# Four graph layers on one core: the first two graphs' layernorm and the linear part of their elu move to VectorE, and a planner gets other durations for transfers

## The chip, the core and the metric

The kernel runs on one core of a Trainium2 chip. The core has five engines that work side by side and each take their instructions in the order in which the program lists them: TensorE (PE: matrix products and transposes into PSUM, with weight loads of its own, PEld), VectorE (DVE), ScalarE (ACT), GpSimd (POOL) and SyncE (SP), which here issues nearly all DMA transfers. The metric is the device time of one execution in microseconds (us), the median of several runs; lower is better.

## The reference

The input is 32 graphs of 512 nodes with 128 features in fp32, and one 512x512 adjacency matrix of zeros and ones that all graphs share. Four residual layers follow each other, each on `h = relu(layernorm(x))`:

```python
# layer 0, on h; the part that the change touches
x_h = elu(h @ Wi + bi)                                  # one 128x512 product a graph
a_src, a_tgt = x_h @ We[:H, 0], x_h @ We[H:, 0]
e = sigmoid(a_tgt[:, :, None] + a_src[:, None, :] + be) * mask
agg = e @ x_h;  self_part = x_h * e.sum(-1)
recv = elu(concat(agg, self_part) @ Wn + bn)
x = x + concat(recv, x_h) @ Wm + bm
# layer 1: five steps of a gated update  h = (1-z) h + z tanh(...), each with adj @ h
# layer 2: x + adj @ (h W) + b
# layer 3: x + sum over k of (adj^k @ h) V_k, k = 0..3
```

## The kernel before

**Layout.** A graph's activations are one tile of 128 features by 512 nodes (or 128 nodes by 4 chunks of 128 features). Graphs are taken in eight groups of four (`G = 4`); layers 0, 1 and 2 are done graph by graph, layer 3 for a group at once. Buffers are numbered slots: 36 SBUF tiles of 128x512 (`f`), and PSUM banks (`b`, eight, of which one is lent to filler work at first).

**The order is written by a planner.** All work is first listed as operations (`op`, line 59) with an engine, a planned duration `us`, a due time, what they read and write, and `result`, the time after its end at which others are thought to see its result (2.5 us for a transfer of SP unless another is given, 0.2 us for the vector engines). `Plan.order` (line 118) then runs through planned time: whenever an engine is free, it takes the ready operation with the earliest due time whose buffers are free. What comes out is a fixed order for each engine, and a fixed slot for each tile. On the chip each engine simply works through its list and waits, with semaphores, for what an instruction needs. A planned duration therefore costs no time itself; it only moves instructions in the lists. A longer `result` puts the consumer later in its engine's list.

**Two plans.** The first covers planned time up to `BRANCH = 18` us (`plan.order(end=BRANCH)`, line 692). In it, when TensorE has nothing ready, a filler product of `ones` by `ones` is written into its list (`plan.idle`, line 301). Then a branch on whether the adjacency matrix is exact in the short format (`inexact`) chooses one of two arms, and the rest is planned for that arm (line 704), without filler.

**The start.** SP issues the loads in the order of their due times: graphs 0 and 1, `Wi`, `bi`, the four chunks of the adjacency matrix, graph 2, and the other weights (lines 313 to 353). The adjacency matrix is transposed, and `mask` is made from it (lines 500 to 531); `n_odd` counts entries that the short format can't hold, and `inexact` is made from the count. In `layernorm` (line 465) VectorE makes the moments (lines 474 to 477), GpSimd the power -1/2 (line 479), VectorE a shift (line 482) and ScalarE, with four instructions of 128x128, `relu(x * scale + shift)` (line 487).

**Layer 0** (`layer0`, line 549), for the first four graphs without DMA: TensorE transposes `h` (line 371), ScalarE copies it from PSUM (line 431), TensorE multiplies by `Wi` (line 442). `elu` (line 534) is three ScalarE instructions on the product, exp (538), tanh (447) and relu (541), and two on VectorE (543, 545). `send` (568) makes messages and scores; `take` (573) and `score` (575) get them out of PSUM; `spread` (605) broadcasts the target scores. Four tanh (620) and four products with `mask` (623) give the attention tiles `es`. They are multiplied by the messages into `pn` (631), and summed over the sources into `ps`: for the first two graphs by four fp32 products with `ones` (line 638, seen at L442), for all others by transfers: SP copies the first tile (641), three accumulating transfers of GpSimd's queue add the others (644), ScalarE and VectorE split the sum in two short parts (648, 649), and TensorE makes the total (654). Then `own` (657), the product with `Wn` (seen at L442), a second `elu`, the output product (667) and the addition to x (462).

Due times in `layer0` are `begin(b)` plus 6, 14, 20, 30 and 44 us; `begin(b)` is 14 us times b for the first four graphs.

Of the kernel before, what the change touches and what calls it, by code (L numbers as in the profile page):

```python
# [13 lines left out]
AF = mybir.ActivationFunctionType  # L14
ALU = mybir.AluOpType

P = 128
# [24 lines left out]
class Plan:  # L42
# [7 lines left out]
    def __init__(self, slots, ahead, last):  # L50
        self.ahead, self.last, self.ops, self.vals = ahead, last, [], {}
        self.free = {k: [(0.0, i) for i in range(n)] for k, n in slots.items()}
        self.until = dict.fromkeys(self.RESULT, 0.0)
        self.shared, self.now = 0.0, 0.0
        self.slack = 0.0
        self.pieces = {}
        self.idle = None
# [60 lines left out]
    def order(self, end=None):  # L118
# [34 lines left out]
        while events:  # L153
# [3 lines left out]
            for e in self.until:  # L157
# [12 lines left out]
                for x in passed:  # L170
                    heapq.heappush(ready[e], x)
                if o is not None and end is not None and any(
                    c.due < o.due and t < now + 0.3 * o.us for t, _, c in coming[e]
                ):
                    heapq.heappush(ready[e], (o.due, index[o], o))
                    o = None
# [37 lines left out]
def tile_four_graph_layers(  # L214
# [97 lines left out]

    def load(v, src, due, us=0.5, to=None, earliest=0.0):
        op("SP", us, due, lambda: nc.sync.dma_start(at(v) if to is None else to(at(v)), src), [], [v],
           earliest=earliest)
        return v

    def load_const(src, shape, name, due, us=0.5, earliest=0.0):
        return load(const(name, shape), src, due, us, earliest=earliest)

    def load_column(src, name, due):
        return load_const(src.rearrange("(p o) -> p o", o=1), [P, 1], name, due, 0.4)

# [5 lines left out]

    def load_graph(b, due):  # L330
        op("SP", 0.65, due, lambda: nc.sync.dma_start(
            at(X[b]), x[b].rearrange("(c p) d -> p c d", p=P)),
            [], [X_group[b // G], X[b]] if b % G == 0 else [X[b]])
# [12 lines left out]
    load(W_tok, Wn[:P], -7, to=lambda t: t[:, :P])  # L346
    load(W_tok, We.rearrange("(t p) o -> p (t o)", p=P), -7, to=lambda t: t[:, P:])
    be_sb = load_const(be.partition_broadcast(P), [P, 1], "be_sb", -7)
    Wn_sb = load_const(Wn[P:], [P, P], "Wn_sb", -6)
    bn_sb = load_column(bn, "bn_sb", -6)  # L350
    Wm_sb = load_const(Wm.rearrange("(t p) o -> p t o", p=P), [P, 2, P], "Wm_sb", -5)
    bm_bc = load_const(bm.partition_broadcast(P), [P, P], "bm_bc", -5, earliest=BRANCH)
    load_graph(3, -6)

# [109 lines left out]

    def layernorm(b, due):
# [25 lines left out]
        op("ACT", 1.56, due, scale, [X[b], s], [h])  # L491
        return h
# [40 lines left out]

    def elu(p, bias, half, due, keep, scale=1.0):

# [13 lines left out]
    def layer0(b, h, due):  # L549
        KEEP = 12  # L550
        if b < G:
            hT = copied(transposed(h, due), due)
        else:
            hT = turned_back(h, due)
            due += 6
        d = due + 6
        xhT = elu(product(Wi_sb, hT, d, blocks=b >= G), bi_sb, bi_half, d, KEEP)

        d = due + 14
        msg, ends = Val("f"), Val("s")  # L560
# [21 lines left out]

        d = due + 20
        row, tgt = Val("d"), Val("f")
# [42 lines left out]

        d = due + 30
        pn = Val("b")
# [49 lines left out]
    def first_layer(b):  # L679
        h = layernorm(b, begin(b))  # L680
        layer0(b, h, begin(b))
# [316 lines left out]
```

## Time and profile before

| what | us |
|---|---|
| median of 3 runs | 1678.89 (1675.96 to 1679.08) |
| the profiled execution | 1678.16 |
| its span in the profile | 1676.4 |
| PE busy | 1662.9 |
| DVE busy | 1420.3 |
| ACT busy | 1130.5 |
| POOL busy | 239.6 |

The profiled execution took 1.8 us more than its span, which is what lies ahead of the first and after the last instruction. It was 0.7 us under the median of the runs. PE's busy time counts the filler too, and matmuls overlap in it, so that a busy PE isn't one that does useful work all the time; where it loses time has to be counted from the starts of its instructions. The granted TensorE clock was 0.999 of full speed.

### The profile page before, as it was taken

To read this page: it belongs to the slowest core of one execution; us is meant where nothing else is said; L and a number is where in the kernel's file an instruction comes from. 1 tells how busy PE (TensorE), PEld (TensorE's weight loads), DVE (VectorE), ACT (ScalarE), POOL (GpSimd) and SP (SyncE) were. 2 spreads that over 40 slices of the span, in tenths; PEclk is the share of its full clock that TensorE was granted. 3 is DMA by queue.
4 is the path that set the end of the run, shared out by engine and by line. 5 is a ranking of instruction groups with operands and counts; after the bars stand their busy time and mean duration, and the time that the engine had idled before them with its cause. 6 is when DMAs were issued, how large, how long until landed. Compare 5 with 4: busy or idle time off the path is not lost.

```text
span 1676.4 us, 21509 instructions
## 1 busy us (share of the span) xinstructions
PE 1662.9 (99%) x6615; PEld 1073.7 (64%) x6615; DVE 1420.3 (85%) x3327; ACT 1130.5 (67%) x2145; POOL 239.6 (14%) x243
## 2 busy tenths in 40 slices
PE   9999999999999999999999999999999999999998
PEld 7555555556666666666666666666666666666797
DVE  6888999999988888889888898888999988877742
ACT  8877677876875676656676676665777767655541
POOL 2311101211111111111101111111121110000110
PEclk9999999999999999999999999999999999999999
DMA  3444424444445434444434444344554543222301
GB/s 108 114 107 138 134 88 138 121 130 115 134 113 138 120 96 127 110 122 131 121 106 111 130 127 127 107 123 109 135 138 122 138 111 103 88 64 88 93 10 53
DMA packets 284157, 188.05 MB, mean 112 GB/s; under 512 B 77312, under 2 KB 236928, under 8 KB 284032
## 3 DMA queue, kind: packets, MB, share of 16 engines
q1 hardware_dynamic: 271072, 162.98, 32.5%
q0 software_dynamic: 12960, 23.60, 8.5%
q8 instruction: 54, 0.88, 0.2%
q14 instruction: 71, 0.58, 0.1%
HBM read 82.25 MB, written 72.81 MB: 92 GB/s over the span
## 4 chain that ended last, share of the span: by engine, by line
PE 62%; DMA 2%; DVE 1%; ACT 0%; issue 0%; SPq 0%; DVEq 0%; POOLq 0%
PE b L442 27%; PE b L821 13%; PE b L911 9%; PE b L902 5%; PE b L631 3%; PE b L667 2%; PE b L884 1%; DMA f<-f 1%; PE b L568 1%; DMA m<-f 1%; PE b L654 1%; DMA f<-m 0%; DVE f L383 0%; SPq L420 0%; ACT f L620 0%
## 5 line engine op out<-in xcount | busy, mean ns | idle before, releaser
L821 PE MATMUL b<-AQ,r 128*128 128x512 f32 x1024 | 303.8, 439 | 0.0
L431 ACT COPY f<-b 128x512 f32<-128x512 f32 x360 | 207.9, 586 | 120.6 <-PE b L821 87.2
L479 POOL TENSOR_TENSOR s<-s,nhalf 128x4 f32<-128x4 f32 x128 | 154.8, 1212 | 822.0 <-DVE s L477 702.6
L821 PEld LDWEIGHTS b<-AQ,r 128*128 128x128 f32 x1024 | 192.3, 188 | 89.3 <-issue 51.5
L846 DVE TENSOR_TENSOR f<-f,b 128x512 f32<-128x512 f32 x320 | 210.9, 676 | 26.6 <-PE b L442 26.2
L911 PE MATMUL b<-r,A_r 128*128 128x512 f32 x768 | 225.0, 427 | 0.0
L383 DVE STREAM_TRANSPOSE f<-f 128x512 f32<-128x512 f32 x244 | 204.7, 843 | 21.2 <-ACT f L487 20.4
L487 ACT ACTIVATE f<-x,s 128x128 f32<-128x128 f32 x512 | 210.5, 490 | 17.4 <-DVE s L482 16.9
L447 ACT ACTIVATE f<-f,b4w 128x512 f32<-128x512 f32 x160 | 115.4, 723 | 144.1 <-DVE f L846 143.5
L911 PEld LDWEIGHTS b<-r,A_r 128*128 128x128 f32 x768 | 139.0, 189 | 46.2 <-issue 24.4
L442 PE MATMUL b<-f,u5T 128*128 128x512 f32 x320 | 163.3, 593 | 1.0 <-DVE f L853 1.0
L442 PE MATMUL b<-f,u3T 128*128 128x512 f32 x320 | 163.3, 593 | 1.0 <-DMA f<-m 1.0
L442 PE MATMUL b<-f,w4T 128*128 128x512 f32 x320 | 162.8, 592 | 0.0
L442 PE MATMUL b<-f,w3T 128*128 128x512 f32 x320 | 162.4, 592 | 0.0
L442 PE MATMUL b<-f,w5T 128*128 128x512 f32 x320 | 162.4, 592 | 0.0
L644 POOL DMA_DIRECT2D f<-f x90 | 80.7, 896 | 536.4 <-DVE f L865 58.1
L821 PE MATMUL b<-A_r,r 128*128 128x512 f32 x512 | 151.9, 438 | 0.0
L863 DVE TENSOR_TENSOR f<-f,f 128x512 f32<-128x512 f32 x160 | 109.2, 683 | 48.9 <-ACT f L447 48.4
L902 PEld LDWEIGHTS b<-V,f 128*128 128x128 f32 x1024 | 131.4, 191 | 25.6 <-issue 19.9
L447 ACT ACTIVATE f<-b,b5w 128x512 f32<-128x512 f32 x160 | 109.4, 684 | 56.0 <-PE b L442 53.5
L447 ACT ACTIVATE f<-f,b3w 128x512 f32<-128x512 f32 x160 | 114.9, 719 | 43.1 <-DVE f L846 42.2
L795 DVE TENSOR_TENSOR r<-f,r 128x512 fp32r<-128x512 f32 x192 | 130.5, 682 | 12.6 <-ACT r L791 12.4
(106 smaller groups left out, 2539.3 us busy)
## 6 DMA issues: line engine op xcount, KB each, us to landing
m<-f SPq DMA_DIRECT2D x244, 256.0 KB, 2.1
f<-m SPq DMA_DIRECT2D x184, 256.0 KB, 2.9
f<-f POOLq DMA_DIRECT2D x90, 256.0 KB, 3.6
f<-m SPq DMA_DIRECT2D x240, 64.0 KB, 2.4
x<-in_x_dram SPq DMA_DIRECT2D x32, 256.0 KB, 3.2
out_dram<-x SPq DMA_DIRECT2D x32, 256.0 KB, 2.5
f<-f SPq DMA_DIRECT2D x30, 256.0 KB, 2.3
f<-d SPq DMA_DIRECT2D x28, 256.0 KB, 5.1
```

The costliest lines, as they stand in the source:

```text
L383: op("DVE", us, due, lambda: nc.vector.transpose(view_out(at(blocks)), view_in(at(src))), [src], [blocks])
L431: op("ACT", us, due, lambda: nc.scalar.copy(at(t), at(src)), [src], [t])
L442: nc.tensor.matmul(to, at(w), of, start=start, stop=stop)
L447: op("ACT", us, due, lambda: nc.scalar.activation(at(dst), at(src), AF.Tanh, bias=at(bias), scale=scale), [src, bias], [dst])
L479: op("POOL", 1.35, due, lambda: nc.gpsimd.tensor_tensor(stat(SCALE), stat(VAR), at(neg_half), op=ALU.pow), [s, neg_half], [s])
L487: nc.scalar.activation(at(h)[:, ts(c, P)], at(X[b])[:, c, :], AF.Relu, bias=stat(SHIFT)[:, c : c + 1], scale=stat(SCALE)[:, c : c + 1],)
L795: op("DVE", T_VEC, due, lambda: nc.vector.tensor_tensor(part(lo), whole(), part(hi).bitcast(F32), op=ALU.subtract), [src, hi], [lo], two=two)
L821: nc.tensor.matmul(at(pa), at(part)[:, ts(jc, P)], view(at(columns)[:, jc, :]), start=jc == n == 0, stop=jc == NC - 1 and n == PARTS - 1,)
L846: op("DVE", T_VEC, d, lambda: nc.vector.tensor_tensor(at(s), at(u), at(pg), op=ALU.add), [u, pg], [s])
L863: op("DVE", T_VEC, d, lambda c=c, h=h: nc.vector.tensor_tensor(at(c), at(c), at(h), op=ALU.subtract), [c, h], [c], two=True)
L902: nc.tensor.matmul(at(pz)[:, ts(i, D)], at(hT[i])[:, ts(ic, P)], at(V[k]), start=i == 0, stop=last and i == G - 1,)
L911: nc.tensor.matmul(at(pz), at(adjT)[:, jc, ts(ic, P)], at(part), start=False, stop=jc == NC - 1 and n == PARTS - 1,)
```

## The change

It has six parts.

1. For graphs 0 and 1 (`FIRST = 2`), `layernorm(relu=False)` leaves out the shift and the four ScalarE instructions; VectorE makes `(x - mean) * scale` in four instructions, and the relu is put into the copy of the transposed tile from PSUM, which stays on ScalarE.
2. In the first `elu` of these two graphs, the linear part `max(p + bias, 0)` is made by VectorE instead of ScalarE.
3. Due times in layer 0 of these two graphs are 0.6 of what they were, and the products with `ones` are due 1 us ahead of the products with the messages. The moments of the first four graphs aren't planned ahead of `begin(b) - 12`.
4. Loads get a shorter time to issue (0.48) and a `result` of their own each.
5. The accumulating transfers get `result=4.6` instead of 3.0, for graphs 2 to 31.
6. In the planner, an operation's ready time is now an event at which the plan looks again, and the rule by which an engine waits for a more urgent operation holds while planned time is under `careful = 18.0` instead of while there is an `end`.

```diff
-                if o is not None and end is not None and any(
+                if o is not None and now < self.careful and any(
                     c.due < o.due and t < now + 0.3 * o.us for t, _, c in coming[e]
...
                             heapq.heappush(coming[a.eng], (a.ready, index[a], a))
+                            heapq.heappush(events, a.ready)
...
+    FIRST = 2
...
+    plan.careful = 18.0
...
-    def load(v, src, due, us=0.5, to=None, earliest=0.0):
+    def load(v, src, due, us=0.5, to=None, earliest=0.0, result=None):
...
-        op("SP", 0.65, due, lambda: nc.sync.dma_start(
+        op("SP", 0.48, due, lambda: nc.sync.dma_start(
...
-    load_graph(0, -9)
-    load_graph(1, -9)
+    load_graph(0, -9, 2.5)
+    load_graph(1, -9, 2.9)
...
-        load(A_nat[ic], adj[ts(ic, P), :], -8, 0.65)
-    load_graph(2, -8)
+        load(A_nat[ic], adj[ts(ic, P), :], -8, 0.48, result=3.9 + 0.2 * ic)
+    load_graph(2, -8, 4.8)
...
-        op("DVE", 1.3, due, moments, [X[b]], [s])
+        op("DVE", 1.3, due, moments, [X[b]], [s], earliest=earliest)
...
-        op("DVE", 0.1, due, lambda: nc.vector.scalar_tensor_tensor(
-            stat(SHIFT), mean(), -1.0, stat(SCALE), op0=ALU.mult, op1=ALU.mult),
-            [s], [s], two=True)
+        if relu:
+            op("DVE", 0.1, due, lambda: nc.vector.scalar_tensor_tensor(
+                stat(SHIFT), mean(), -1.0, stat(SCALE), op0=ALU.mult, op1=ALU.mult),
+                [s], [s], two=True)
...
+        def normed():
+            for c in range(NC):
+                nc.vector.tensor_scalar(
+                    at(h)[:, ts(c, P)], at(X[b])[:, c, :], mean()[:, c : c + 1],
+                    stat(SCALE)[:, c : c + 1], op0=ALU.subtract, op1=ALU.mult)
+        if relu:
+            op("ACT", 1.56, due, scale, [X[b], s], [h])
+        else:
+            op("DVE", 0.9, due, normed, [X[b], s], [h])
...
-        op("ACT", T_ACT, due, lambda: nc.scalar.activation(
-            at(r), at(p), AF.Relu, bias=at(bias), scale=scale), [p, bias], [r])
+        if relu_by_vector:
+            assert scale == 1.0
+            op("DVE", T_VEC, due, lambda: nc.vector.tensor_scalar(
+                at(r), at(p), at(bias), 0.0, op0=ALU.add, op1=ALU.max), [p, bias], [r])
+        else:
+            op("ACT", T_ACT, due, lambda: nc.scalar.activation(
+                at(r), at(p), AF.Relu, bias=at(bias), scale=scale), [p, bias], [r])
...
-            hT = copied(transposed(h, due), due)
+            pt, hT = transposed(h, due), Val("f")
+            op("ACT", T_COPY, due, lambda pt=pt: nc.scalar.activation(
+                at(hT), at(pt), AF.Relu if b < FIRST else AF.Copy), [pt], [hT])
...
-        d = due + 6
-        xhT = elu(product(Wi_sb, hT, d, blocks=b >= G), bi_sb, bi_half, d, KEEP)
-
-        d = due + 14
+        pace = 0.6 if b < FIRST else 1.0
+        d = due + 6 * pace
+        xhT = elu(product(Wi_sb, hT, d, blocks=b >= G), bi_sb, bi_half, d, KEEP,
+                  relu_by_vector=b < FIRST)
+
+        d = due + 14 * pace
...
-        d = due + 20
+        d = due + 20 * pace
...
-        d = due + 30
+        d = due + 30 * pace
...
-                product(ones, es[jc], d, ps, start=jc == 0, stop=jc == NC - 1)
+                product(ones, es[jc], d - 1, ps, start=jc == 0, stop=jc == NC - 1)
...
-                   two=False, result=3.0)
+                   two=False, result=4.6)
...
-        recv = elu(pn, bn_sb, bn_half, d + 6, 2, ALPHA / 2)
-
-        d = due + 44
+        recv = elu(pn, bn_sb, bn_half, d + 6 * pace, 2, ALPHA / 2)
+
+        d = due + 44 * pace
...
-        h = layernorm(b, begin(b))
+        h = layernorm(b, begin(b), relu=b >= FIRST, earliest=begin(b) - 12.0 if b < G else 0.0)
```

The other loads get their `result` in the same way (W_tok 4.5, be 4.3, Wn 4.0, bn 3.6, graph 3 3.6), and columns are issued in 0.48 instead of 0.4.

More of the change, by code (lines that the diff above doesn't have):

```diff
@@ L54, in __init__ @@
         self.shared, self.now = 0.0, 0.0
+        self.careful = 0.0
         self.slack = 0.0
@@ L310, in tile_four_graph_layers, with load_const, load_column @@
         at(warm)[:, :1], at(ones)[:, :1], AF.Tanh), [ones], [warm])
-    def load(v, src, due, us=0.5, to=None, earliest=0.0):
+    def load(v, src, due, us=0.5, to=None, earliest=0.0, result=None):
         op("SP", us, due, lambda: nc.sync.dma_start(at(v) if to is None else to(at(v)), src), [], [v],
-           earliest=earliest)
+           earliest=earliest, result=result)
         return v
[L318 to L322, printed above, removed]
+    def load_const(src, shape, name, due, us=0.5, earliest=0.0, result=None):
+        return load(const(name, shape), src, due, us, earliest=earliest, result=result)
+    def load_column(src, name, due, result=None):
+        return load_const(src.rearrange("(p o) -> p o", o=1), [P, 1], name, due, 0.48, result=result)
     X_group = [Val("x") for _ in range(NG)]
@@ L328, in tile_four_graph_layers, with load_graph @@
     plan.vals.update(dict.fromkeys([*X_group, *X]))
-    def load_graph(b, due):
-        op("SP", 0.65, due, lambda: nc.sync.dma_start(
+    def load_graph(b, due, result=None):
+        op("SP", 0.48, due, lambda: nc.sync.dma_start(
             at(X[b]), x[b].rearrange("(c p) d -> p c d", p=P)),
-            [], [X_group[b // G], X[b]] if b % G == 0 else [X[b]])
-    load_graph(0, -9)
-    load_graph(1, -9)
+            [], [X_group[b // G], X[b]] if b % G == 0 else [X[b]], result=result)
+    load_graph(0, -9, 2.5)
+    load_graph(1, -9, 2.9)
     Wi_sb = load_const(Wi, [P, P], "Wi_sb", -9)
@@ L340, in tile_four_graph_layers @@
     for ic in range(NC):
-        load(A_nat[ic], adj[ts(ic, P), :], -8, 0.65)
-    load_graph(2, -8)
+        load(A_nat[ic], adj[ts(ic, P), :], -8, 0.48, result=3.9 + 0.2 * ic)
+    load_graph(2, -8, 4.8)
     W_tok = const("W_tok", [P, P + 2])
-    load(W_tok, Wn[:P], -7, to=lambda t: t[:, :P])
+    load(W_tok, Wn[:P], -7, to=lambda t: t[:, :P], result=4.5)
     load(W_tok, We.rearrange("(t p) o -> p (t o)", p=P), -7, to=lambda t: t[:, P:])
-    be_sb = load_const(be.partition_broadcast(P), [P, 1], "be_sb", -7)
-    Wn_sb = load_const(Wn[P:], [P, P], "Wn_sb", -6)
-    bn_sb = load_column(bn, "bn_sb", -6)
+    be_sb = load_const(be.partition_broadcast(P), [P, 1], "be_sb", -7, result=4.3)
+    Wn_sb = load_const(Wn[P:], [P, P], "Wn_sb", -6, result=4.0)
+    bn_sb = load_column(bn, "bn_sb", -6, result=3.6)
     Wm_sb = load_const(Wm.rearrange("(t p) o -> p t o", p=P), [P, 2, P], "Wm_sb", -5)
     bm_bc = load_const(bm.partition_broadcast(P), [P, P], "bm_bc", -5, earliest=BRANCH)
-    load_graph(3, -6)
+    load_graph(3, -6, 3.6)
     def scaled(v, factor, name, due):
@@ L463, in add_to_x, with layernorm @@
         op("DVE", T_VEC, due, add, [X[b], p], [X[b]], two=two)
-    def layernorm(b, due):
+    def layernorm(b, due, relu=True, earliest=0.0):
         s, h = Val("s"), Val("f")
@@ L490, in scale @@
                 )
-        op("ACT", 1.56, due, scale, [X[b], s], [h])
+        def normed():
[7 more added lines that the diff above has]
+            op("DVE", 0.9, due, normed, [X[b], s], [h])
         return h
@@ L531, in tile_four_graph_layers, with elu @@
        [p_odd], [inexact])
-    def elu(p, bias, half, due, keep, scale=1.0):
+    def elu(p, bias, half, due, keep, scale=1.0, relu_by_vector=False):
         e, t, r = Val("f"), Val("f"), Val("f")
```

## The prediction, made before the changed kernel was run

> **What bounds the kernel now.** I read the busy time of the engines first, then TensorE's waits, then the waits of the engines that feed it, then the first 60 us as a timeline and by stretches. The page's first part:
>
> ```profile
> PE 1662.9 (99%) x6615; PEld 1073.7 (64%) x6615; DVE 1420.3 (85%) x3327; ACT 1130.5 (67%) x2145; POOL 239.6 (14%) x243
> ```
>
> TensorE is the bound, but its busy time holds filler and overlap. So I count useful work: an fp32 product with 512 columns is two matmul records 0.429 us apart, a record in the short format 0.231, a 128-column fp32 record 0.112 (differences of starts in the timeline). Over all rows but the filler this makes 1643.0 us. Up to a time t, the lost time is t less the useful work begun by then: 15.3 us at 20, 16.1 at 25, 16.4 at 45, 17.1 at 55, 18.3 at 100, 27.0 at 1600. After the last matmul come 6.4 us (last addition, store). So only two things can give time back: 18 us at the start, and scattered stalls, which the waits of TensorE name:
>
> ```profile
> PE b L654 <- DVE q L649: 2.8, 5, 0.9
> PE b L301 <- DVE ones L296: 1.0, 1, 1.0
> PE b L442 <- DVE f L853: 1.0, 2, 0.6
> PE b L442 <- DMA f<-m: 1.0, 1, 1.0
> PE b L631 <- DVE f L623: 0.6, 1, 0.6
> PE b L442 <- DVE f L657: 0.5, 2, 0.3
> ```
>
> The largest is the total of the attention tiles, which waits for the accumulating transfers by way of two engines. The same wait on those engines, in the list for all engines:
>
> ```profile
> ACT q L648 <- DMA f<-f: 29.9, 19, 4.9
> ...
> DVE q L649 <- ACT q L648: 16.3, 13, 2.6
> ```
>
> In 19 of 30 graphs ScalarE stands still for the last accumulation, and all that is listed behind L648 stands too. The transfers (last row on L644) land in
>
> ```profile
> DMA to landing us min/median/max: 3.2/3.6/4.9
> ```
>
> The start by stretches (columns: PE, PEld, DVE, ACT, POOL busy, clock, DMA):
>
> ```profile
> 10.00:20.00 10.00, 10.00 (x90) 9.37 (x90) 8.03 (x30) 8.37 (x19) 1.90 (x4) 1.00 0.09 21
> 20.00:30.00 10.00, 9.36 (x38) 4.95 (x37) 7.21 (x31) 9.87 (x24) 3.69 (x8) 1.00 0.53 138
> 30.00:40.00 10.00, 9.90 (x39) 5.48 (x38) 8.38 (x21) 10.00 (x24) 1.04 (x1) 1.00 0.22 68
> ```
>
> From 20 to 40 us ScalarE is full (9.87, 10.00): it feeds TensorE there. Before that, TensorE's timeline:
>
> ```profile
> 9.60 0.72 PE L301 MATMUL b<-ones 128*128 128x128 f32 x5
> 10.16 1.47 PE L513 MATMUL b<-ident,f 128*128 128x128 f32 x12
> 11.47 0.60 PE L371 MATMUL b<-ident,f 128*128 128x128 f32 x4
> ```
>
> The first 31 fillers end at about 10.1 us, and real work waits for them in the list: the last chunk of the adjacency matrix landed at 9.0, and graph 0's `h` was done at 9.8 (L487, 8.14 plus 1.64).
>
> **What the Trainium skill says.** "TensorE: Matmul & The Clock Gate", Architectural detail: ScalarE's and VectorE's queues are strict FIFO. The trace agrees: L648's 29.9 us. "ScalarE: Activation LUTs", What ACT_TABLE_LOAD costs: an ACTIVATE with a pointer operand takes about 280 + 0.833 N ns, 93 more for a second one, and neighbours overlap by 93, so an estimate of 0.39 us for each step of L487; in the trace four stand in 1.55 us (25.08 to 26.63), the same. "VectorE: DVE Perf Modes", The TRN2 errata: (58 + N/2)/0.96 ns for fp32 `tensor_scalar` in SBUF at double rate, (120 + N)/0.96 from PSUM at single rate. "DMA: Bandwidth & Descriptors", Anatomy of one DMA: 2.0 us + bytes/436e3, an estimate of 2.6 us for 256 KB from GpSimd; the trace has 3.6, and the trace decides.
>
> **The change, part by part.**
>
> *Off ScalarE.* For two graphs L487 (2 x 1.55) and L541 (2 x 0.57 start to start): 4.2 us, and two L482 (0.15 each) off VectorE. *Onto VectorE:* eight 128x128 `tensor_scalar`, which the trace hasn't got. From below, the skill's price (58 + 64)/0.96 = 127 ns each, 0.5 us a graph; from above the nearest row, L474 at 0.87 for four. I take 0.8. For the relu the price is 0.66, the row L543 0.69, 0.61 start to start. The relu in the copy costs nothing: the same instruction count, 0.59 as L431. Nothing here is on the path at first: VectorE is done with graph 0 at about 7.1 us (pow ends at 6.15), while fillers cover TensorE until 10.1, as they cover 9.8 now. Without them it would save 2.7 us. What is listed behind the new VectorE steps, the checks of the adjacency chunks, waits for ScalarE's casts until 7.6 anyway.
>
> *Order at the start.* The changed program lists 55 fillers (53 before, 0.22 us each), the first 31 again ahead of everything, then graph 0's transposes before the adjacency ones. I laid its lists end to end with the durations above (0.47 for a copy on ScalarE, 0.57 for exp or tanh, 0.58 a tanh of the attention, 0.61 on VectorE, 1.27 for moments, 0.2 from VectorE or ScalarE to TensorE), each instruction starting when its engine and its inputs allow:
>
> - Graph 0: transposes 10.16 (11.47 now), `Wi` product 11.7 (13.0), messages 16.4 (17.1; five fillers stand ahead of them), target scores 18.3 (19.9), first tanh of the attention 18.9 (20.6). A lead of 1.6 us.
> - Then the lists spend it. Graph 1's `Wi` product, at 20.4 now, stands behind the four products with `ones` (20.7 to 24.1, as fast as VectorE delivers) and starts at 24.1. ScalarE, done with graph 1's copy at 21.8, has nothing until 25.2: 3.4 idle us in the stretch that it fills now, of the 4.2 that it was relieved of.
> - First stall: graph 1's scores go to the bank that holds graph 0's `pn`, which ScalarE reads last at 31.46; TensorE is there at 30.6, starts at 31.66: 1.05 us. Second: the output product of graph 0 waits for its second `elu`, whose last VectorE step stands behind moments of two later graphs and ends at 34.4; TensorE is there at 32.9, starts at 34.6: 1.7. Third: graph 0's first product of layer 1 goes to the bank that graph 2's relu reads until 47.3; TensorE is there at 46.6: 0.9.
> - At 53.8 us the useful work begun is 34.4: lost 19.4, against 17.0 or 17.1 now. So +2.3 us, and I take no more until 100 us, as now 1.3 is lost there. The method may be off by 2 us either way: ScalarE's list is the chain, and 0.05 us on each of its 60 instructions makes 3.
>
> *Loads as planned.* SP's list keeps its first 16 transfers in the same order, so nothing lands at another time. `inexact` is made about 3 us sooner (16 instead of 19.1), so the loads behind the branch (now from 20.3) go about 3 us sooner, too, into an idle queue: no cost; nothing waits for them.
>
> *Accumulation, 4.6 instead of 3.0.* Three accumulations follow each other: planned 3 x (1.0 + 3.0) = 12.0 us, now measured steps of 4.05 and 3.77 (issues at 49.54, 53.59, 57.36), in the tail up to 4.9 + 0.5 each. Planned after: 16.8. In the listed order, the useful TensorE work between a graph's scores and its L654 grows from 29 to 35 us at the least, 32.5 to 38 in the middle. The worst stall now is 1.02 us (at 640.8), so 4.8 more cover all. That removes L654's later stalls, counted from starts with the next instruction's delay: 0.75 (323.6), 0.73 (386.0), 0.38 (581.3), 1.02 (640.8), 0.65 (1147.1), and 0.43 on the product after it (643.2): 3.96. Buffers are held 4.8 us longer in a queue of 36; the listed work shows no thinner place.
>
> *New event.* It lets the plan start work up to 0.3 us sooner, all through. The gates of layer 1 get tighter: the useful work between the w4 and u5 products, with add, tanh and multiply (L846, L447, L853) between, is at most 3.6 us in 12 places instead of 5. A stall there costs 0.75 (at 633.1). I take +0.7. The `careful` edit changes nothing, as both hold exactly in the first plan.
>
> Sum: +2.3 - 4.0 + 0.7 = -1.0, on the profiled 1678.16: 1677.2; that execution stands 0.7 under the median, so I say 1677.5. A measurement of this kernel can tell about 0.2%, 3.4 us.
>
> **Rivals.**
>
> *The start pays as meant.* ScalarE is full from 20 to 40 us, so 4.2 us less there could all come back as TensorE time: -4.2 - 3.3 = -7.5, 1670.7; half of it, 1674.2. For it: the first graph's lead of 1.6 us. Against: the 3.4 us hole behind the `ones` products.
>
> *The gates of layer 1 take it all.* 0.75 us for each tight place: if the 7 more all stall, +5.3, and with the start +2.3 and -4.0: +3.6, 1681.8. It decides from seven on (+3.4 with rounding). For it: VectorE is 85% busy and its list is in order. Against: of the five places now, the two stalls seen (62.5 and 633.1, 1.3 us) are not at the tightest.
>
> *The later sum doesn't help, since `own` and the `Wn` product move along with it.* The distance from L654 to the product is 1.7 us as before. Then only the start stays, +2.3 to +3: 1680.5 to 1681, still same. Against: that distance is as short now, and only two of the 30 products stalled.
>
> **How the numbers follow.** The mixed outcome (near nothing, the last rival with it) 0.52; the start pays 0.28; the gates or a worse start 0.20. Its own range is 1675.0 to 1681.5. To hold eight in ten I reach to most of the first rival, 1671.0, and past the second, 1683.5.
>
> **What would show it.** Right: L654 missing from TensorE's waits after 100 us, L648's 29.9 us down to a few; ScalarE idle about 3 us between 21 and 26 us; stalls at L628 (scores), L690 (output product) and L844 (layer 1), by the changed file's lines, between 30 and 50 us; lost time near 19 at 55 us. Wrong: graph 1's `Wi` product before 22 us; no stall until 50; or waits on L876 (now L853) summing to over 3 us.

## The result, and the profile after

The changed kernel takes 1681.91 us (median; 1680.43 to 1683.72), the kernel before 1678.09 on the same chip: a ratio of 1.0023, with a 95% interval of 1.0015 to 1.0032. The forecast was 1677.5, so the time lies within the range on record, but some 4 us above the forecast: the kernel became a little slower instead of staying as it was. The profiled execution has a span of 1679.9 us (1676.4 before). Useful TensorE work is the same 1643.0 us in both; all that moved is lost time. The first part of the page of the changed kernel shows TensorE at 99% again, with 1.7 us less "busy" although the kernel is slower, which is why lost time is counted from the starts of matmuls:

```profile
PE 1661.2 (99%) x6619; PEld 1075.8 (64%) x6619; DVE 1424.3 (85%) x3335; ACT 1127.9 (67%) x2135; POOL 236.9 (14%) x243
```

Lost time (t less the useful work begun by t, as in the prediction), by stretch:

| stretch | before | after | difference | predicted |
|---|---|---|---|---|
| to 55 us | 17.1 | 18.9 | +1.8 | +2.3 |
| 55 to 100 us | 1.2 | 3.1 | +1.9 | 0 |
| 100 to 400 us | 3.7 | 6.4 | +2.7 | |
| 400 to 1600 us | 5.0 | 1.8 | -3.2 | -3.3 for both stretches |

The tail behind the last matmul is 0.8 us longer (7.2 against 6.4), and 0.4 less is lost between 1600 us and it. The waits of TensorE in the changed kernel (total us, times, longest), to be read against those of before: the attention total, there the largest with 2.8 us in five places, is left with one wait (L677, at 78 us, in graph 2). Line numbers moved with the change: the total is L654 in the kernel before and L677 in the changed one (L655 and L676 in some files below), while L654 of the changed kernel is the product of the attention with the features. That product and the u3 product (L447 with L890; u3, u5 and w4 are products of layer 1's gated steps) stand in the total's place:

```profile
PE b L654 <- DVE f L646: 2.3, 2, 1.8
PE b L447 <- DVE f L890: 2.0, 1, 2.0
PE b L628 <- ACT f L560: 1.7, 1, 1.7
PE b L447 <- DMA f<-m: 1.3, 1, 1.3
PE b L677 <- DVE q L672: 1.1, 1, 1.1
...
PE b L844 <- ACT f L560: 0.7, 1, 0.7
PE b L690 <- DVE f L564: 0.6, 1, 0.6
```

L628, L844 and L690 are the three stalls of the start that the prediction named. ScalarE's wait for the accumulating transfers, 29.9 us before, is gone from the list altogether; VectorE's wait behind it fell from 16.3 us to

```profile
DVE q L672 <- ACT q L671: 3.9, 6, 0.8
```

The start on TensorE's timeline (start, length, line; in brackets the idle time and what ended it). Graph 1's first product, behind eight records with `ones`, begins at 24.05, and the three stalls follow at 32.36, 34.37 and 47.33:

```profile
20.61 3.60 PE L447 MATMUL b<-f,ones 128*128 128x512 f32 x8
24.05 1.02 PE L447 MATMUL b<-f,Wi_sb 128*128 128x512 f32 x2
...
32.36 0.65 PE L628 MATMUL b<-ident,s 128*128 128x128 f32 x4 [1.67 <-ACT f L560]
...
34.37 2.05 PE L690 MATMUL b<-Wm_sb,f 128*128 128x128 f32 x16 [0.58 <-DVE f L564]
...
47.33 2.14 PE L844 MATMUL b<-A_r,r 128*128 128x512 f32 x8 [0.74 <-ACT f L560]
```

ScalarE's timeline shows the pause foretold (3.39 us), and a second wait that was not:

```profile
25.11 0.69 ACT L552 ACTIVATE f<-b,bi_sb 128x512 f32<-128x512 f32 x1 [3.39 <-PE b L447]
26.62 0.69 ACT L452 ACTIVATE f<-b,bi_half 128x512 f32<-128x512 f32 x1 [0.82 <-DVE f L557]
```

L452 reads the bank that L557, the new relu on VectorE, reads as well. Here the two readers went one after the other.

Further on, the largest new stall is the one at 330.37 us on a u3 product, 2.15 us. VectorE's timeline ahead of it (start, length, line):

```profile
327.18 0.71 DVE L388 STREAM_TRANSPOSE f<-f 128x512 f32<-128x512 f32 x1
327.81 0.65 DVE L888 SCALAR_TENSOR_TENSOR f<-f,f 128x512 f32<-128x512 f32 x1
328.38 0.86 DVE L479 BATCH_NORM_STATS2 s<-x 128x6 f32<-128x128 f32 x4
329.15 0.36 DVE L481 BATCH_NORM_AGGREGATE s<-s 128x2 f32<-128x6 f32 x4
329.55 0.17 DVE L482 TENSOR_SCALAR s<-s 128x4 f32<-128x4 f32 x1
329.63 0.68 DVE L890 SCALAR_TENSOR_TENSOR f<-f,f 128x512 f32<-128x512 f32 x1
```

TensorE waits for L890. One transposition and the moments of another graph stand in the list ahead of it, on an engine without a gap. Nothing of this is an edit of the change; it is the order that came out. The question for the experiments is therefore how much of the result belongs to the parts, and how much to the order in which the planner happened to put what they left alone.

### The profile page after: what moved, and what is told of

Its sections match the earlier page's. It is cut to its first block, busy times and chain, and to the rows that moved or that the text cites. A ratio compares the mean times of both kernels' runs of the same rounds, so it can differ in the third digit from the quotient of the medians.

```text
span 1679.9 us, 21519 instructions
## 1 busy us (share of the span) xinstructions
PE 1661.2 (99%) x6619; PEld 1075.8 (64%) x6619; DVE 1424.3 (85%) x3335; ACT 1127.9 (67%) x2135; POOL 236.9 (14%) x243
## 4 chain that ended last, share of the span: by engine, by line
PE 89%; DVE 6%; DMA 2%; ACT 2%; issue 1%; SPq 0%; POOL 0%; DVEq 0%; POOLq 0%; ACTq 0%
PE b L447 40%; PE b L844 19%; PE b L934 10%; PE b L925 6%; PE b L654 6%; PE b L690 3%; PE b L907 1%; PE b L591 1%; DVE f L388 1%; DMA f<-m 1%; PE b L305 1%; DMA m<-f 1%; PE b L677 1%; ACT f L493 1%; DVE f L869 1%
## 5 line engine op out<-in xcount | busy, mean ns | idle before, releaser
L844 PE MATMUL b<-AQ,r 128*128 128x512 f32 x1024 | 302.7, 438 | 0.2
L484 POOL TENSOR_TENSOR s<-s,nhalf 128x4 f32<-128x4 f32 x128 | 150.9, 1182 | 928.6 <-DVE s L482 791.8
L844 PEld LDWEIGHTS b<-AQ,r 128*128 128x128 f32 x1024 | 191.8, 188 | 88.7 <-issue 47.4
L493 ACT ACTIVATE f<-x,s 128x128 f32<-128x128 f32 x504 | 206.7, 488 | 26.3 <-DVE s L488 25.9
L452 ACT ACTIVATE f<-f,b4w 128x512 f32<-128x512 f32 x160 | 115.4, 724 | 157.0 <-DVE f L869 156.2
L447 PE MATMUL b<-f,u3T 128*128 128x512 f32 x320 | 163.3, 593 | 3.3 <-DVE f L890 2.0
L447 PE MATMUL b<-f,w4T 128*128 128x512 f32 x320 | 163.0, 593 | 0.0
L447 PE MATMUL b<-f,w5T 128*128 128x512 f32 x320 | 162.6, 592 | 0.0
L447 PE MATMUL b<-f,u5T 128*128 128x512 f32 x320 | 162.4, 592 | 0.0
L447 PE MATMUL b<-f,w3T 128*128 128x512 f32 x320 | 162.3, 592 | 0.0
L844 PE MATMUL b<-A_r,r 128*128 128x512 f32 x512 | 149.4, 434 | 0.7 <-ACT f L560 0.7
L452 ACT ACTIVATE f<-b,b5w 128x512 f32<-128x512 f32 x160 | 109.4, 684 | 54.4 <-PE b L447 52.6
L452 ACT ACTIVATE f<-f,b3w 128x512 f32<-128x512 f32 x160 | 115.0, 719 | 35.5 <-DVE f L869 34.6
```

The lines of the kernel that those rows point to most:

```text
L447: nc.tensor.matmul(to, at(w), of, start=start, stop=stop)
L452: op("ACT", us, due, lambda: nc.scalar.activation(at(dst), at(src), AF.Tanh, bias=at(bias), scale=scale), [src, bias], [dst])
L484: op("POOL", 1.35, due, lambda: nc.gpsimd.tensor_tensor(stat(SCALE), stat(VAR), at(neg_half), op=ALU.pow), [s, neg_half], [s])
L493: nc.scalar.activation(at(h)[:, ts(c, P)], at(X[b])[:, c, :], AF.Relu, bias=stat(SHIFT)[:, c : c + 1], scale=stat(SCALE)[:, c : c + 1],)
L844: nc.tensor.matmul(at(pa), at(part)[:, ts(jc, P)], view(at(columns)[:, jc, :]), start=jc == n == 0, stop=jc == NC - 1 and n == PARTS - 1,)
```

## The experiments

Two theories go in. **A**: each part of the change (the start with its loads; the longer accumulation; the new event) has a cost of its own, and they add up. **B**: any edit of the plan's numbers redraws the whole order behind it, and the stalls of that order are a draw; then a part's own effect shows only over several orders. Two narrower ones come up in some expectations. **C**: it is the new event that makes the change slower. **D**: the longer accumulation takes out whatever stalls of the total an order has, and nothing else. All times are medians; the kernel before, run beside each, had 1677.5 to 1679.0. Ratios have 95% intervals.

**The accumulation alone.**

```diff
-                   two=False, result=3.0)
+                   two=False, result=4.6)
```

> The kernel before with 4.6 us planned for an accumulating transfer, nothing else changed. By the parts (theory A: each part of the change has a cost of its own, and they add up): the stalls of the attention total (L654 of this file) after 300 us are gone, the start up to 55 us is as before (17.1 us lost), and the time is 3 to 4 us shorter, about 1674.5. By the reshuffle (theory B: every edit of the plan's times redraws the order of everything behind it, and the stalls of the new order are drawn anew): the total's stalls are gone, but others of 0.5 to 2 us each, on other lines, take their place, and the time lies anywhere from 1675 to 1681.

Measured: 1675.05 us, ratio 0.9984 (0.9978 to 0.9991). No stall of the total after 100 us (3.5 us in five places before); lost from 400 us on 0.4 us against 5.0. But from 100 to 400 us it loses 5.1 against 3.7: one new stall of 3.33 us on L821 at 327.8 us. So the part does what it says, and a part of the gain went to a new place.

**The new event alone**, one line:

```diff
                             heapq.heappush(coming[a.eng], (a.ready, index[a], a))
+                            heapq.heappush(events, a.ready)
```

> The kernel before with the new event alone: the plan may begin an operation when its inputs are ready, not at the next other event. By A: it makes what the changed kernel lost more between 100 and 400 us (6.4 us there, 3.7 before), so about 1681, with stalls of 1.5 to 2 us on the u3 product in that stretch, and 5 us lost after 400 us as before. By B: 1675 to 1681, and its losses are not gathered between 100 and 400 us.

Measured: 1688.41, ratio 1.0059 (1.0046 to 1.0072). Its losses are spread (6.8 us from 55 to 100, 6.9 to 400, 6.1 after), which neither theory's number covers (about 1681, and 1675 to 1681).

**The start alone** (the changed kernel less the other two parts).

```diff
-                            heapq.heappush(events, a.ready)
-                   two=False, result=4.6)
+                   two=False, result=3.0)
```

> The changed kernel without the new event and with 3.0 us for an accumulation: only what concerns the first two graphs and the loads. By A: 18.9 us lost at 55 us and 21.9 at 100 (17.1 and 18.3 before), so 3.6 us longer, 1681.7, with the stalls of the total after 300 us as before. By B: 1.8 us more at 55 us, since that is fixed by the lists of the start, but after it anything from -2 to +3, so 1678 to 1683, and the 1.3 us stall of graph 2's total at 78 us may be missing. If the start costs nothing by itself, 1678, and the events at 24 us are due to the new event.

Measured: 1681.62, ratio 1.0035 (1.0023 to 1.0048); 19.3 us lost at 55, 21.1 at 100, and 4.4 us of stalls of the total after that. A's number, and its start.

**A shuffle**: one planned duration 0.3% longer.

```diff
-    T_VEC, T_COPY, T_ACT, T_DMA = 0.61, 0.5, 0.6, 0.45
+    T_VEC, T_COPY, T_ACT, T_DMA = 0.612, 0.5, 0.6, 0.45
```

> The kernel before with 0.612 in place of 0.61 us planned for one VectorE step: no work, wait or transfer is changed, only the plan's numbers by 0.3%, and the order after 55 us comes out different. By A: the time stays within 1 us of 1678, with the total's stalls after 300 us as before, and as much lost in each stretch. By B: it moves by 1 to 3 us, either way, with stalls at other places and on other lines; then a difference of this size tells nothing of a part by itself.

Measured: 1691.17, ratio 1.0078 (1.0065 to 1.0091). It is slower than the whole change by 9 us, and no instruction does anything else than before. This is the clearest reading of the study. Its waits of TensorE, against 2.8 us in five places on L654 before:

```profile
PE b L654 <- DVE q L649: 9.3, 9, 2.1
PE b L442 <- ACT f L431: 2.0, 1, 2.0
PE b L442 <- DVE f L853: 1.4, 3, 0.5
```

Theory A in its strict form is gone: the sum of the parts measured singly (-2.75, +10.6, +3.8) is +11.7, the change is +3.8. B holds, with a spread of 13 us where I had thought of 3. But the draw isn't blind: half of the 13 us that this order loses more are further stalls of the total (9.3 us of waits against 2.8), which the longer accumulation is made to remove.

**Parts by pairs, and the shuffle with the accumulation.** e_start_sum is the changed kernel without the event; e_start_event has 3.0 again; e_event_sum is the kernel before with event and 4.6; n_shuffle1_sum is the shuffle with 4.6.

> The changed kernel without the new event: the start and the 4.6 us for an accumulation. If the new event is what costs (C: the event makes the start's loss and the saving of the sum come out at +3.8 instead of less), then the start's own 1681.6 less the total's stalls that the start alone still showed after 100 us (4.4 us on the sum's line): about 1677. If the parts add up as measured one by one (A: +3.8 and -2.75): 1678.9. If each order is a new draw (B): anything from 1675 to 1690, and the sum's stalls gone but for one or two.

Measured: 1676.94, ratio 0.9988 (0.9980 to 0.9996). This is C's number: without the event the changed kernel is 1.8 us faster than the kernel before, with it 3.8 slower. The next runs ask whether that is the event or the draw.

> The changed kernel with 3.0 us for an accumulation: the start and the new event. A (the parts add up, +3.8 and +10.6): 1692. B: 1680 to 1692, with five or more stalls of the attention total after 100 us, 3 to 10 us in all, as in the four orders with 3.0 seen so far (4.0 in the kernel before, 4.4, 6.0 and 10.6).

Measured: 1684.44, ratio 1.0037 (1.0025 to 1.0049), with three stalls of the total after 100 us, 2.9 us.

> The kernel before with the new event and 4.6 us for an accumulation. A (+10.6 and -2.75): 1685.6. D (the longer time takes out whatever the order had of stalls at the total, 6.0 us with the event alone, and the two on the product behind it, 1.7): 1680.5 to 1682.5, with at most one such stall after 100 us. B: 1675 to 1690.

Measured: 1673.60, ratio 0.9969 (0.9958 to 0.9980), better than D said.

> The kernel with 0.612 for a VectorE step (1691.2 by itself) with 4.6 us for an accumulation. D: its stalls of the total, 10.6 us in nine places, go: 1680 to 1681.5, lost time after 400 us down from 7.4 to under 2. A: the gain is that of the sum alone, 2.75: 1688.4. B: anywhere from 1675 to 1691; a time within 3 us of the kernel with the sum alone (1675.1) would say that 4.6 holds whatever the order, and that the spread of orders comes mostly from the total's stalls.

Measured: 1673.78, ratio 0.9972 (0.9961 to 0.9983). The stalls of the total are gone: the order that was 13 us slower is now 5 faster than the kernel before. So the longer accumulation is worth 2.75 us on the kernel before, 4.7 with the start, 2.5 with start and event, 14.8 with the event and 17.4 on the shuffled order (differences of medians, partly of different chips, where the kernel before itself stood 1 us apart). The event cost 10.6 by itself and gains 1.5 once 4.6 stands (1675.05 to 1673.60); with the start it costs 2.8, and with start and 4.6 5.0 (1676.94 to 1681.91). An effect that changes its sign with the order isn't a price of the event, but C is not shut out for the kernels that have the start: only one of their orders with 4.6 is without the event. The waits of TensorE with the event and 4.6 (L632, L443 and L302 are the lines of before, moved by one) have no total left in them:

```profile
PE b L632 <- DVE f L624: 1.4, 2, 1.0
PE b L443 <- ACT f L432: 1.1, 2, 0.7
PE b L302 <- DVE ones L297: 1.0, 1, 1.0
PE b L443 <- DVE f L854: 0.3, 1, 0.3
```

**What of the start costs.** Three kernels each undo one thing in the changed kernel, and a fourth shuffles it.

```diff
 s_ones_d
-                product(ones, es[jc], d - 1, ps, start=jc == 0, stop=jc == NC - 1)
+                product(ones, es[jc], d, ps, start=jc == 0, stop=jc == NC - 1)
 s_pace1
-        pace = 0.6 if b < FIRST else 1.0
+        pace = 1.0
 s_relu_act
-                  relu_by_vector=b < FIRST)
+                  relu_by_vector=False)
 n_after_shuffle
-    T_VEC, T_COPY, T_ACT, T_DMA = 0.61, 0.5, 0.6, 0.45
+    T_VEC, T_COPY, T_ACT, T_DMA = 0.612, 0.5, 0.6, 0.45
```

> The changed kernel with the four products with ones due with the others of the attention (d instead of d - 1). If the loss at the start comes from their standing ahead of graph 1's first product (hole theory): that product begins at 20 to 21 us instead of 24.05, ScalarE's pause of 3.4 us before 25 us falls under 1.5, and the lost time at 55 us falls from 18.9 to 17 or less. If it comes from the new order of the banks and of VectorE as a whole: the three stalls (scores at 32.4, output product at 34.4, first layer-1 product at 47.3; 3.4 us in all) or others of this size stay, and 18.5 to 19.5 us are lost at 55. The time: 1681.9 less what is won there, if what follows were the same; as the order behind it is drawn anew, 1672 to 1681, without a stall of the attention total after 100 us.

Measured: 1682.80, ratio 1.0023 (1.0015 to 1.0030). Graph 1's product begins at 22.02, with two of the four attention products (L654) ahead of it, ScalarE's pause is 1.67 us, and yet 19.8 us are lost at 55. The hole theory falls as the sole cause: with the pause halved, a stall of 2.08 us at 34.95 takes the place of those at 32 and 34.

> The changed kernel with pace 1.0 for the first two graphs: the layernorm and relu on VectorE and the planned loads stay, the sooner due times go. If the sooner due times are what costs (hole theory): graph 1's first product at about 20 us, no pause of ScalarE over 1.5 us, lost at 55 us 17 or less, so below the kernel before by what ScalarE is relieved of. If what was taken from ScalarE and put on VectorE costs: 18.5 or more at 55 us, with stalls behind VectorE. The time: 1672 to 1681, no stall of the total after 100 us.

Measured: 1679.91, ratio 1.0004 (0.9996 to 1.0012). Graph 1's product at 21.01, 17.9 us lost at 55: more than half of the loss is gone. But 6.8 us are lost from there to 100.

> The changed kernel with the relu of the first two graphs' elu on ScalarE again. The plan then lists graph 1's first product ahead of the products with ones. If the two readers of one bank (ScalarE's exp and tanh, VectorE's relu, one after the other by their semaphores) or VectorE's list cost: lost at 55 us falls from 18.9 to about 17. If only the hole costs, it falls as much, but graph 1's product at under 22 us shows it. If the relief of ScalarE by 1.1 us is worth something, 19 to 20. The time: 1672 to 1683, no stall of the total after 100 us.

Measured: 1678.91, ratio 0.9999 (0.9991 to 1.0008). Graph 1's product at 17.58, and 19.5 us lost at 55. Neither the hole nor the two readers of one bank carry the loss.

> The changed kernel with 0.612 in place of 0.61 us planned for one VectorE step. If what it loses from 55 to 400 us (9.5 us, against 4.9 before) belongs to the parts of the change (A), those losses and the time stay within 1 us: 1681 to 1683, with stalls of 1.5 to 2 us at 263, 330 and 341 us. If it is the draw of the order (B), they are redrawn: 18.9 lost at 55 us again, but the stalls between 55 and 400 us are others, and the time lies where the other orders with 4.6 lie with 1.8 us for the start on top, 1675 to 1679.

Measured: 1679.84, ratio 1.0004 (0.9995 to 1.0012). At 55 us again 18.9, with the same three stalls (L628, L690, L844): the start's loss is fixed by its lists. Behind it, everything is redrawn: 1.9 us lost from 100 to 400 (6.4 in the change), 0.1 after, but 6.7 from 55 to 100. Its waits of TensorE begin with a u5 product that the changed kernel had no wait on, and have a larger one on a Wn product (L680, 0.5 there); L628 is the start's, L677 graph 2's total:

```profile
PE b L447 <- DVE f L876: 2.8, 1, 2.8
PE b L628 <- ACT f L560: 1.7, 1, 1.7
PE b L677 <- DVE q L672: 1.4, 1, 1.4
PE b L447 <- DVE f L680: 1.3, 1, 1.3
```

So the stalls of 263, 330 and 341 us in the changed kernel belong to its draw, not to a part. The time is a draw as well: the same six parts are 3.8 us slower than the kernel before in one order and 0.9 in the other, and the second interval holds no difference at all.

**Further into the start, and the size of the time.** The next kernels set FIRST to 0 (nothing moved to VectorE, due times as before; the planned loads, earliest times, `ones` due time, event and 4.6 stay), shuffle that, and take the earliest times away too. Two others give 3.8 us to an accumulation in the kernel before, and shuffle that; one more shuffles the kernel before with 4.6.

```diff
 s_first0, s_first0_shuffle (the latter with T_VEC 0.612), s_first0_noearliest
-    FIRST = 2
+    FIRST = 0
 s_first0_noearliest
-        h = layernorm(b, begin(b), relu=b >= FIRST, earliest=begin(b) - 12.0 if b < G else 0.0)
+        h = layernorm(b, begin(b), relu=b >= FIRST, earliest=0.0)
 n_sum_act (with result=4.6)
-    T_VEC, T_COPY, T_ACT, T_DMA = 0.61, 0.5, 0.6, 0.45
+    T_VEC, T_COPY, T_ACT, T_DMA = 0.61, 0.5, 0.602, 0.45
 e_sum38, e_sum38_shuffle (the latter with T_VEC 0.612)
-                   two=False, result=3.0)
+                   two=False, result=3.8)
```

> The changed kernel with FIRST = 0: layernorm and relu of the first two graphs on ScalarE and their due times as before; the planned loads, the earliest times, the ones products' due time, the new event and the 4.6 us stay. If the work moved to VectorE and the sooner due times make the loss at the start: 17 to 17.6 us lost at 55 us and 1672 to 1677, as the three orders with 4.6 and no edit of the start (1673.6 to 1675.1). If the planned loads or the ones products make it: 18.9 or more at 55 us, and 1676 to 1683, as the five orders that have the start.

Measured: 1679.48, ratio 1.0006 (0.9998 to 1.0014); 18.6 us lost at 55, 7.1 more to 100.

> The same with 0.612 in place of 0.61 us planned for a VectorE step, a second draw of the order: the lost time at 55 us within 0.5 us of the run before, and the time within 4 us of it either way. If FIRST makes the loss, both lie under 1677.

Measured: 1680.99, ratio 1.0021 (1.0015 to 1.0028); 18.6 and 7.6. So the work on VectorE and the sooner due times aren't the whole loss either. The waits of TensorE in s_first0:

```profile
PE b L447 <- DVE f L890: 2.5, 1, 2.5
PE b L447 <- DVE f L876: 2.2, 2, 1.5
PE b L447 <- DVE f L680: 1.9, 1, 1.9
```

The first stands at 71 us and most of the second (1.66 us) at 83: stalls of layer 1's first steps, between 55 and 100 us. The third is of the draw, at 1160 us.

> The changed kernel with FIRST = 0 and without the earliest times of the layernorms, so that VectorE takes graph 2's moments ahead of the attention, as in the kernel before. If the earliest times make the loss at the start: 17 to 17.6 us lost at 55 us, under 20.5 at 100, without the stalls of 2.7 and 1.7 us at 71 and 82 us, and 1672 to 1676. If the ones products ahead of the scores' product make it: 18.5 or more at 55 us, and 1676 to 1682.

Measured: 1678.59, ratio 1.0005 (0.9996 to 1.0013); 19.9 us at 55, 26.0 at 100. Not the earliest times. What is left with FIRST at 0 is the `ones` products ahead of the scores' product and the loads, and neither was run by itself. (The event and 4.6 stay as well, but lose only 17 us by 55 in e_event_sum.)

> The kernel before with 4.6 us for an accumulation and 0.602 in place of 0.6 us planned for a ScalarE step, one more draw of the order. If orders with 4.6 and without the start's edits lie below those with them: 1672.5 to 1676. If the three seen were lucky draws: 1676 to 1682. No stall of the attention total after 100 us in either case.

Measured: 1675.29, ratio 0.9981 (0.9972 to 0.9990).

> The kernel before with 3.8 us for an accumulation, between 3.0 and 4.6. The accumulations land 3.6 us after their issue in the middle and 4.9 at most, and three follow each other: planned 14.4 us, measured 13 or so. If the middle landing is what must be covered: no stall of the total after 100 us, 1673 to 1678. If the slow landings decide: two to four such stalls of 0.3 to 1 us remain, 1676 to 1682.

Measured: 1670.92, ratio 0.9953 (0.9940 to 0.9967), the fastest of all. The waits of TensorE over its whole execution:

```profile
PE b L631 <- DVE f L623: 2.2, 3, 1.1
PE b L301 <- DVE ones L296: 1.0, 1, 1.0
PE b L654 <- DVE q L649: 0.3, 1, 0.3
```

> The kernel before with 3.8 us for an accumulation and 0.612 in place of 0.61 us planned for a VectorE step. If 3.8 does as well as 4.6 and the 1670.9 was one good draw: 1671 to 1676, no stall of the attention total after 100 us. If 3.8 is too short once the order is another: two or more such stalls, 1676 to 1684 (the same order's edit with 3.0 has 9.7 us of them and 1691.2).

Measured: 1673.41, ratio 0.9974 (0.9964 to 0.9985), with one stall of the total after 100 us, 0.68. So 3.8 does as well as 4.6, and part of the 1670.9 was a good draw.

All orders together, lost time in us by stretch (means over the orders of a row; the times are those given above):

| orders | times | to 55 | 55 to 100 | 100 to 400 | 400 to 1600 |
|---|---|---|---|---|---|
| 3.0 for an accumulation (5, the kernel before among them) | 1678 to 1691.2 | 17.1 to 19.3 | 3.7 | 5.7 | 5.5 |
| 3.8 or 4.6, no edit of the start (6) | 1670.9 to 1675.3 | 17.1 | 2.2 | 3.0 | 0.5 |
| 4.6, the start's edits in whole or part (9, the changed kernel among them) | 1676.9 to 1682.8 | 19.1 | 5.6 | 3.0 | 1.5 |

Every order of the second row is faster than the kernel before, and every one of the third slower than all of the second. By 55 us the start's edits cost 2.0 us, without the event too (19.3 in e_start, 19.7 in e_start_sum). From 55 to 100 us the third row loses 3.4 more, but this isn't shown to be the start's alone: eight of its nine orders have the event, the ninth loses 3.5, and e_event and n_shuffle1 lose 6.8 and 5.9 there without any edit of the start. The longer accumulation saves 4 to 5 us after 400 and some 3 from 100 to 400.

Six pairs of kernels differ by a null edit alone (a planned duration 0.3% longer). In the one pair with 3.0 it moved the median by +13.4 us; in the five with 3.8 or 4.6 by -2.1, -1.3, +0.2, +1.5 and +2.5. The wide spread was seen only where the accumulation was planned at 3.0.

## Why the prediction was right or wrong

**The start to 55 us, +2.3: right.** Measured +1.8, and 1.8 to 2.6 in the other orders with the whole start. The places were as laid out: graph 1's product at 24.05 (24.1), the pause 3.39 (3.4). The three stalls, from starts, are 1.81, 0.73 and 0.89 us (1.05, 1.7 and 0.9): the first was longer, as ScalarE's last read of the bank (L560) ended at 32.30 and not at 31.46. TensorE came that much later to the second, which was shorter, since VectorE's step behind it ended where it was laid out (34.31, for 34.4). So the sum held. But the cause that I read out of these, the product standing behind `ones`, was not shown by the runs; it fell in s_ones_d and s_relu_act. Laying out the lists gave the sum, not the reason. No single edit that was undone brought the loss back to 17.1, so what makes it stays open; nearest came the due times (17.9 without pace 0.6).

**"I take no more until 100 us": the first step that failed.** It is +1.9 us in the changed kernel; the nine orders with the start lose 3.4 us more there, in the mean, than the six without (with the reserve above on the event). I had laid the lists out to 54 us and put down for the rest what the kernel before loses. In the trace it is 1.31 us on graph 2's total at 78.04 (L671 waits on ScalarE behind L452, which stood 2.30 us for TensorE), 0.65 on L654 at 94 and 0.30 on L844; in seven of the other eight orders the largest stall there is one of 1.4 to 2.95 us on a u3 or u5 product. Why the start's edits should bring these is open.

**The accumulation, -4.0: right in place, and in what it takes out of the kernel before.** The five stalls that I summed are gone (3.5 us after 100 us, without the 0.4 on the product behind the total), and with 3.8 or 4.6 there is one such stall after 100 us in fifteen orders. By itself it gave -2.75, as the new order brought a stall of 3.33 us. I took its worth from the kernel before alone; the other orders with 3.0 have 2.9 to 9.7 us of these stalls, and there it is worth up to 17.4.

**The new event, +0.7: the second step that failed, by its mechanism.** No gate of layer 1 (L876) stalls in the changed kernel, though I had counted twelve tight places. The 2.7 us more from 100 to 400 us hide a larger sum: the total's two stalls there (1.5 us) went, and the u3 stall of 1.15 us with them; 1.92, 2.15 and 1.48 us on L654 and u3 came. n_after_shuffle, with the same parts, has none of the three. They are the draw of a new order. So from 100 to 1600 us, where accumulation and event were to save 3.3 us, the change saved 0.5. A term for the reshuffle was missing from the sum: not a price of +0.7 but a spread, which n_shuffle1 showed as 13.4 us with 3.0 and which the six orders with the longer time and no edit of the start show as 4.4.

**The rivals.** The start did not pay in any order. "The gates take it all" has the number (1681.8), but not the mechanism: the wait that it rests on isn't there. (It is there once with the same parts: 2.8 us on L876 at 98.8 us in n_after_shuffle, again by the draw.) The later sum did help.

**The signs and the sum.** Every sign named for "right" came, none of those for "wrong", and the direction was wrong all the same: no sign counted the time lost from 55 to 400 us, which grew by 4.6 us. A slip besides: 1677.2 with the 0.7 between execution and median makes 1677.9, not 1677.5.

**Single prices.** Four L499 take 1.11 us from start to end (0.8 taken; outside the bounds of 0.5 to 0.87), L557 0.75 (0.69). The price that the prediction took from the Trainium skill ("VectorE: DVE Perf Modes", The TRN2 errata: 127 ns a step, 0.5 us for the four) is under half of what the trace shows for the four, and the trace decides. The same section warns that this row is too low for single operations and puts the fixed term nearer 150 cycles, which the prediction left out; with that, an estimate of 0.22 us a step or 0.9 for the four comes nearer. No wait of TensorE leads to these steps: VectorE was done with graph 0's at 7.4 us, and TensorE's transposes began at 9.98; graph 1's ended at about 19.7, when ten fillers ahead of its transposes ran out. The serial reading of one bank (0.57 and 0.82 us on ScalarE) was not in my working.

## What to carry to other kernels

Where a planner writes the order, as here, a change's effect is its own effect plus a new draw of everything behind it. Price the second from a few null edits of the plan's numbers before reading a difference of this size as the effect of a part; and judge a part by several orders that have it against several that don't. A planned time a little above the middle landing of a transfer (here 3.8 us, for 3.6 to 3.7 measured) took the bad draw of n_shuffle1 away without covering the slowest landings, and so was worth more than the stalls of one profile say.

## What the runs showed of the hardware that was not expected

**A stall can be paid twice.** After a stall of 2 us or more of TensorE the granted clock sometimes fell for some microseconds. The kernel with the accumulation alone, around its stall of 3.33 us that ends at 327.77 (columns: stretch, length, busy PE, PEld, DVE, ACT, POOL, granted clock, DMA):

```profile
326.00:328.00 2.00, 0.23 (x1) 0.23 (x2) 1.97 (x11) 2.00 (x6) 0.80 (x1) 0.98 0.82 258
328.00:330.00 2.00, 2.00 (x6) 1.52 (x6) 1.91 (x3) 2.00 (x5) 0.61 (x1) 0.50 0.40 65
330.00:332.00 2.00, 2.00 (x6) 1.37 (x5) 1.91 (x4) 1.93 (x5) 0.00 (x0) 0.67 0.83 215
332.00:334.00 2.00, 2.00 (x8) 1.21 (x7) 1.49 (x3) 1.35 (x4) 0.00 (x0) 1.00 0.44 152
```

At 0.50, the records that follow stand some 0.2 us further apart than elsewhere: 1.7 us in all, on top of the stall. In the twenty profiled executions, 17 stalls were of 2.0 us or more; 11 of them were followed by a clock of 0.57 to 0.69 over the next 4 us, six by 1.00 (one of 2.71 us among these, so length alone doesn't decide). The three largest of the changed kernel were not followed by a fall.

**The transfers land later at worst than one profile said**: 6.9 us at most in the changed kernel against 4.9 before, with 3.7 in the middle. Over all twenty profiles the middle is 3.5 to 3.8 us, the slowest of 90 landings 4.8 to 8.2. A plan with 3.8 served nevertheless in both orders that had it (one stall of 0.68 us). That three transfers follow each other, so that their planned sum counts and not the slowest one, is my reading; it was not tried.
